# Moving DVE and GpSimd work around a stage boundary, and re-pacing the last stage of a two-layer graph kernel

## The chip, the core and the metric

The kernel runs on one core of a Trainium2 chip. The core has a matrix engine (TensorE, PE in the profile; its weight loads are a row of their own, PEld), three elementwise engines (VectorE = DVE, ScalarE = ACT, GpSimd = POOL) and SyncE (SP), which only issues DMAs. Each engine takes its instructions strictly in order, and an instruction that waits holds up everything behind it on its engine. The metric is the device time of one execution in microseconds (us); lower is better. All arithmetic is float32.

## The reference

Sixteen graphs (B = 16) of 1024 nodes with 256 channels go through two layers, each followed by a residual and a layernorm. Cut to what matters here:

```python
# layer 0
Wg  = adj * similarity(mean over channels)          # 1024 x 1024 per graph
q   = relu((x^T @ Wg) * para)^T ; k, v = split(x @ kv_w)
x1  = layernorm(x + softmax(q k^T * scale) v)       # 4 heads of 64
# layer 1
A   = adj + I
deg = A.sum(0) + A.sum(1) - diag(A) ; dinv = rsqrt(deg)
A_hat = A * dinv[:, None] * dinv[None, :]
agg = A_hat @ x1                                     # the same A_hat for all graphs
h   = relu(batchnorm(agg @ W1.T + b1))               # statistics over all 16*1024 rows
o   = batchnorm(h @ W2.T + b2)
out = layernorm(x1 + o)
```

The two batchnorms cut the kernel into stages: nothing behind one of them can start before the last graph is in front of it.

## The kernel before, in words

A general path stands behind a range check of the softmax denominators and does not run here; the profile is that of `fast_path`. Its stages:

1. **Attention** (to 1692 us). 512 units (graph b, head pair, query half qh, key block m), two units to a "burst", 16 bursts to a graph (u = 0 to 15 in the code). A unit's `scores` are PE matmuls (L926) into a PSUM tile `ps`, ACT's exponential (L931) makes `p` from it, `outputs` are PE matmuls (L947) with `p`, and DVE sums the eight `p` of a group into `acc` (L955 for the first pair, L957 after that). `p` has four buffers, so the exponential of unit i waits for PE and DVE to be done with the `p` of unit i-4. After the eighth unit of a group ACT copies one half of the result (L964) and DVE adds the other half from PSUM (L965, `oT`). A head pair's results are then normalised and added to x (`residual`: DVE L998, PE L1004, DVE L1008, POOL L1013).
2. **The last graph** has no next graph to prepare. Its bursts carry the preparation of A_hat instead, in the table `last`, keyed by u: the adjacency is transposed into eight tiles `ahT` (u = 0 to 7), the degrees and dinv are made (u = 9; dinv goes to DRAM and comes back as a row copied to all partitions, `dinv_row`, L1102 and L1104 on SP), the identity is added on POOL (u = 12, L1109), and `scale_adjacency(m)` multiplies a tile by its column and row of dinv on DVE (L1112). Tiles 0 and 1 are scaled at u = 14, tile 2 inside the last `outputs`, tiles 3 to 7 behind it.
3. **The first aggregate** (`aggregate_first`, L1139, 1695 to 1732 us): for m = 0 to 7, four matmuls into four PSUM banks, of which the two of c = 0 are the banks that the last attention group's `po` had: their first writes wait for L964 and L965. A float32 matmul shows as two instructions. Woven in are `adjacency_sums` (DVE, L693 to L696, four sums per block for the seven-product scheme that the other fifteen graphs use), the last denominators (L977) and the last residuals.
4. **Aggregates and first linear layer** (to 2290 us): seven-product matrix multiplication, paced by PE. Its operands are the sums `aT`, `x1S` (POOL `left_sums`, L686 to L689, one set for each graph) and `wS` (the same helper on W1, once).
5. **Second linear layer** (L1541, to 2515 us): 16 graphs in two halves c of 128 channels. DVE (L1569) or, for the very last half, ACT (L1564) adds the bias b2 and moves the result from PSUM to `o2T`; DVE takes batchnorm statistics from `o2T` (L1573). After the last graph `coefficients2(c)` aggregates them (L1305), DVE and POOL make scale and shift (L1306 to L1310, with POOL's power at L589).
6. **The end** (2515 to 2611 us), a loop over graphs in which `residual2(b)` is PE transposes and additions (L1614, L1629, L1646) with DVE additions and statistics (L1634, L1636, L1652), then the layernorm's ten small instructions (`coefficients`: seven on the engine given, three on POOL); `scale_shift(b)` applies the second batchnorm in place on ACT (L1605); `finish(b)` applies the layernorm on ACT and DVE (L1686, L1680) and stores (L1695 on SP; the last graph in two halves, L1692 on SP and L1693 on ACT's queue). Half of each graph's sum stays in PSUM in one of three `held` buffers until ACT has read it in `finish`. In iteration b come `residual2(b)`, `scale_shift(b + 2)`, `finish(b - 1)`.

PE, ACT and DVE execute in the order in which the code is written. POOL and SP do not: there the tile framework's planner simulates the program and puts each instruction where it finds it ready, program order deciding only between those ready together. In the trace the identity additions, written at u = 12, run on POOL from 1624 us on, between residuals written before and after them.

Of the kernel before, what the change touches and what calls it, by code (L numbers as in the profile page):

```python
# [18 lines left out]
P = 128  # L19
# [496 lines left out]
def fast_path(  # L516
# [43 lines left out]
    def tile_s(name):  # L560
        return psum["s"].tile([P, N], F32, tag="s", name=name)
# [165 lines left out]
    with (  # L727
# [430 lines left out]
        with tc.manual_schedule(engines={mybir.EngineType.PE, mybir.EngineType.Activation, mybir.EngineType.DVE}):  # L1158
# [35 lines left out]
            for u, todo in (  # L1194
                (1, (load_weights,)), (6, (load_x1l, 0)), (9, (degrees,)),
                (10, (transpose_weights, 0)), (11, (transpose_weights, 1)),
                (12, (add_identity,)), (14, (scale_adjacency, 0)),
                (14, (scale_adjacency, 1)),
            ):
                last.setdefault(u, []).append((todo[0], todo[1:]))  # L1200
            for i in range(4):
# [91 lines left out]

    w1T, w2T = wl["w1T"], wl["w2T"]

    def batchnorm(stats, gamma, beta, k, name, eng=nc.gpsimd):


        mv = const.tile([P, k, 2], F32, name=f"{name}_mv")
        sg = const.tile([P, k], F32, name=f"{name}_sg")  # L1300
        sh = const.tile([P, k], F32, name=f"{name}_sh")

        def coefficients(j):
            g, s = sg[:, j : j + 1], sh[:, j : j + 1]
            nc.vector.bn_aggr(mv[:, j, :], stats[:, j].rearrange("p a s -> p (a s)"))  # L1305
            eng.tensor_scalar(g, mv[:, j, 1:2], EPS, None, ALU.add)  # L1306
            rsqrt(g, g, 0.0)
            eng.tensor_tensor(g, g, gamma[:, j : j + 1], ALU.mult)
            eng.tensor_tensor(s, mv[:, j, 0:1], g, ALU.mult)
            eng.tensor_tensor(s, beta[:, j : j + 1], s, ALU.subtract)  # L1310

        return coefficients, sg, sh
# [8 lines left out]
    with (  # L1321
# [9 lines left out]
        def temps(k):  # L1331
# [4 lines left out]

        wS = strt.tile([P, 4, C], F32, name="wS")
        F0, F1 = slice(0, C), slice(C, FH)
        left_sums(
            nc.gpsimd, [wS[:, i, :] for i in range(4)],  # L1340
            w1T[:, 0, F0], w1T[:, 1, F0], w1T[:, 0, F1], w1T[:, 1, F1],
        )

        x1S = {}

# [95 lines left out]
                steps.pop(0)()  # L1441

        x1_sums(1)
        lin = linear1(0)
        for b in range(1, B):
            if 1 < b < B - 1:
# [64 lines left out]
    with tc.tile_pool(name="hl", bufs=2) as hl, tc.tile_pool(name="o2p", bufs=1) as o2p:  # L1511
# [7 lines left out]
            xf[b] = pool.tile([P, NCH, C], F32, tag=tag, name=f"xf_{b}")  # L1519
            nc.sync.dma_start(xf[b], x1_d[b])  # L1520

        coefficients2, sg2, sh2 = batchnorm(bn2_st, cols["g2"], cols["be2"], CC, "bn2", nc.vector)
        hs_of = {0: h0}

        def load_h(b):
# [5 lines left out]
        for b in range(B):  # L1531
            if b + 2 < B:
                load_h(b + 2)
            if b + 1 < B:
                for k in range(HC):
                    scale_shift1(hs_of[b + 1][k], k)
            h = hs_of.pop(b)
            pss = [tile_s(f"po2_{b}_{c}") for c in range(CC)]

            def mm(c, k, hs):  # L1540
                nc.tensor.matmul(  # L1541
                    pss[c][:, hs], w2T[:, k, c * P : (c + 1) * P], h[k][:, hs],
                    start=(k == 0), stop=(k == HC - 1),
                )

            if b == 0:

                for ks in (range(HC // 2), range(HC // 2, HC)):
                    for c in range(CC):
                        for k in ks:  # L1550
                            for hs in (H0, H1):
                                mm(c, k, hs)
            for c in range(CC):
                ps = pss[c]
                last = b == B - 1 and c == CC - 1
                if b:
                    for k, hs in (
                        [(k, hs) for hs in (H0, H1) for k in range(HC)] if last
                        else [(k, hs) for k in range(HC) for hs in (H0, H1)]
                    ):  # L1560
                        mm(c, k, hs)
                if last:
                    for hs in (H0, H1):
                        nc.scalar.activation(  # L1564
                            o2T[b][:, c, hs], ps[:, hs], AF.Identity,
                            bias=cols["b2"][:, c : c + 1],
                        )
                else:
                    nc.vector.tensor_scalar(  # L1569
                        o2T[b][:, c, :], ps, cols["b2"][:, c : c + 1], None, ALU.add  # L1570
                    )
                for half, hs in enumerate((H0, H1)):
                    nc.vector.bn_stats(bn2_st[:, c, 2 * b + half, :], o2T[b][:, c, hs])  # L1573
                if b == B - 1:
                    coefficients2(c)
            if b >= B - 3:
                load_x1(b - (B - 3), xp, "x")
# [7 lines left out]
        with (  # L1585
# [34 lines left out]
            def residual2(b):  # L1620
                xt = xf[b]
                last = b == B - 1
                st = small.tile([P, NCH, 6], F32, tag="ln_st", name=f"st_l1_{b}")
                for pair in range(2):
                    pt = ps_sum.tile([P, HALF], F32, tag="sum", name=f"pf_{b}_{pair}")
                    for j in range(2):
                        n = 2 * pair + j
                        for c in range(CC):
                            nc.tensor.transpose(  # L1629
                                pt[:, j * C + c * P : j * C + (c + 1) * P],  # L1630
                                o2T[b][:, c, n * P : (n + 1) * P], ident,
                            )
                    xs = xt[:, 2 * pair : 2 * pair + 2, :].rearrange("p n c -> p (n c)")
                    nc.vector.tensor_add(xs, pt, xs)  # L1634
                    for n in (2 * pair, 2 * pair + 1):
                        nc.vector.bn_stats(st[:, n, :], xt[:, n, :])  # L1636
                if last:
                    first = coefficients(b, st, M0, nc.vector)
                for pair in range(2, 4):
                    if b:  # L1640
                        add_x1(b, pair)
                    pt = held[b][:, (pair - 2) * HALF : (pair - 1) * HALF]
                    for j in range(2):
                        n = 2 * pair + j
                        for c in range(CC):
                            nc.tensor.matmul(  # L1646
                                pt[:, j * C + c * P : j * C + (c + 1) * P],
                                o2T[b][:, c, n * P : (n + 1) * P], ident,
                                start=False, stop=True, skip_group_check=True,
                            )  # L1650
                for n in range(4, NCH):
                    nc.vector.bn_stats(st[:, n, :], held[b][:, (n - 4) * C : (n - 3) * C])  # L1652
                if last:
                    return first, coefficients(b, st, M1, nc.vector)
                return (coefficients(b, st, slice(0, NCH), nc.gpsimd),) * 2

            def coefficients(b, st, ns, pool):

# [15 lines left out]
            def finish(b, *coeffs):  # L1674
                xt, hx = xf.pop(b), held.pop(b)
                y = o2T[b].rearrange("p c n -> p (c n)").rearrange("p (n c) -> p n c", c=C)
                last = b == B - 1
                for n in (0, 1, 2, 3, 7) if last else (0, 1):
                    rstd, nmr = coeffs[n // 4]
                    nc.vector.tensor_scalar(  # L1680
                        y[:, n, :], hx[:, (n - 4) * C : (n - 3) * C] if n >= 4 else xt[:, n, :],
                        rstd[:, n : n + 1], nmr[:, n : n + 1], ALU.mult, ALU.add,
                    )
                for n in (4, 5, 6) if last else (4, 5, 6, 7, 2, 3):
                    rstd, nmr = coeffs[n // 4]
                    nc.scalar.activation(  # L1686
                        y[:, n, :], hx[:, (n - 4) * C : (n - 3) * C] if n >= 4 else xt[:, n, :],
                        AF.Identity, bias=nmr[:, n : n + 1], scale=rstd[:, n : n + 1],
                    )
                dst = out[b].rearrange("(n p) c -> p n c", p=P)  # L1690
                if last:
                    nc.sync.dma_start(dst[:, M0, :], y[:, M0, :])  # L1692
                    nc.scalar.dma_start(dst[:, M1, :], y[:, M1, :])  # L1693
                else:
                    nc.sync.dma_start(dst, y)  # L1695
                if b in (4, 6):
                    load_x1_pair(b + 6)
                elif b + 7 < B and not 3 <= b < 7:
                    load_x1(b + 7, xp, "x")
# [6 lines left out]
            coeffs = {}  # L1706
            for b in range(B):
                coeffs[b] = residual2(b)
                if b + 2 < B:
                    scale_shift(b + 2)  # L1710
                if b:
                    finish(b - 1, *coeffs.pop(b - 1))
            finish(B - 1, *coeffs.pop(B - 1))
# [43 lines left out]
```

## Time and profile before

| | us |
|---|---|
| median of 3 runs | 2611.93 (2611.75 to 2612.31) |
| profiled execution | 2612.64 |
| its span, first to last instruction | 2610.6 |
| PE busy in the span | 2561.6 (98%) |
| DVE / ACT / POOL busy | 1518.4 / 1201.1 / 356.6 |
| stage borders | attention to 1692, first aggregate to 1732, aggregates and linear 1 to 2290, linear 2 to 2515, end to 2611 |

How to read it. The granted PE clock is 0.996 over the span and falls visibly in two places: 1701 to 1708 us, and behind the last matmul. In the stretch 1692 to 1732 PE is busy for 36.6 of 40.0 us at a mean clock of 0.91; in the end, 73.9 of 96.0 us. Everywhere else in the kernel PE has hardly a gap, so an edit on another engine can only matter where PE waits for that engine, or where PE has no work left.

### The profile page before, as it was taken

How to read it: one execution, taken by the hardware profiler on the slowest of the kernel's cores; microseconds unless marked ns; L12 is line 12 of the kernel's file. 1: busy time of each engine (PE TensorE's matmuls, PEld its weight loads, DVE VectorE, ACT ScalarE, POOL GpSimd, SP SyncE). 2: the span in 40 equal slices, each digit the busy share in tenths (PEclk: the TensorE clock that was granted, in tenths of full speed). 3: DMA queues.
4: the chain of work that ended last, by engine and by line, in shares of the span. 5: the costliest groups of instructions: out<-in, count | busy, mean ns of one | idle time of the engine just before them, and what ended most of it. 6: DMA issues, size and time to landing. Idle time of an engine off the chain costs nothing.

```text
span 2610.6 us, 32351 instructions
## 1 busy us (share of the span) xinstructions
PE 2561.6 (98%) x13158; PEld 1127.4 (43%) x13158; DVE 1518.4 (58%) x1966; ACT 1201.1 (46%) x1478; POOL 356.6 (14%) x427
## 2 busy tenths in 40 slices
PE   9999999999999999999999999999999999999997
PEld 5443443444434434444344344344444444444455
DVE  5375665655756656557566566665655656443368
ACT  6365564664655646646556464611101111143358
POOL 0010110101101101011011010332211222000026
PEclk9999999999999999999999999999999999999999
DMA  4001101011011010110110101022212222254449
GB/s 145 1 10 41 33 10 41 18 26 33 10 41 34 9 41 19 24 33 10 41 34 9 41 19 32 12 79 97 97 65 97 81 97 85 102 200 161 160 165 337
DMA packets 134574, 168.97 MB, mean 65 GB/s; under 512 B 86800, under 2 KB 120080, under 8 KB 124048
## 3 DMA queue, kind: packets, MB, share of 16 engines
q1 hardware_dynamic: 129056, 115.95, 14.3%
q0 software_dynamic: 4832, 50.34, 4.6%
q8 instruction: 105, 1.72, 0.3%
q10 hardware_dynamic: 528, 0.52, 0.1%
q14 instruction: 53, 0.43, 0.1%
HBM read 99.36 MB, written 67.44 MB: 64 GB/s over the span
## 4 chain that ended last, share of the span: by engine, by line
PE 86%; DVE 9%; ACT 3%; issue 1%; DMA 0%; POOL 0%; DVEq 0%; POOLq 0%; ACTq 0%
PE ps L926 16%; PE po L947 16%; PE pg L829 16%; PE po L1541 8%; PE pv L879 5%; PE b_agg L1371 4%; PE c_agg L1371 4%; PE pk L866 3%; PE a_agg L1371 2%; PE b_h L1403 2%; PE c_h L1403 2%; PE pxT L790 1%; PE den L977 1%; PE a_h L1403 1%; PE pagg L1139 1%; PE pg L851 1%
## 5 line engine op out<-in xcount | busy, mean ns | idle before, releaser
L931 ACT ACTIVATE p<-ps 128x1024 f32<-128x1024 f32 x512 | 496.8, 1024 | 183.9 <-PE ps L926 152.6
L957 DVE TENSOR_TENSOR acc<-acc,p 128x1024 f32<-128x1024 f32 x384 | 487.4, 1269 | 122.4 <-ACT p L931 94.1
L926 PE MATMUL ps<-qT,kT 64*64 64x512 f32 x4096 | 490.8, 592 | 0.7 <-DVE qT L838 0.3
L947 PE MATMUL po<-p,v 64*64 64x512 f32 x4096 | 487.9, 589 | 0.0
L829 PE MATMUL pg<-wg,x 128*128 128x512 f32 x960 | 420.9, 594 | 0.0
L1013 POOL TENSOR_TENSOR x<-x,o 128x512 f32<-128x512 f32 x64 | 122.2, 1910 | 1164.7 <-DVE o L1008 1164.7
L947 PEld LDWEIGHTS po<-p,v 64*64 64x64 f32 x4096 | 160.0, 133 | 280.2 <-issue 271.3
L829 PEld LDWEIGHTS pg<-wg,x 128*128 128x128 f32 x960 | 178.9, 190 | 221.5 <-issue 208.5
L926 PEld LDWEIGHTS ps<-qT,kT 64*64 64x64 f32 x4096 | 152.0, 133 | 281.5 <-issue 250.4
L1541 PE MATMUL po<-hl,w12T 128*128 128x512 f32 x512 | 220.0, 592 | 0.8 <-ACT hw L1493 0.8
L838 DVE SCALAR_TENSOR_TENSOR qT<-pg,para_s 128x1024 f32<-128x1024 f32 (+1 forms) x34 | 39.2, 1161 | 236.2 <-PE pg L829 234.9
L819 DVE SCALAR_TENSOR_TENSOR wg<-wg,adj_s 128x1024 f32<-128x1024 f32 x128 | 162.1, 1278 | 21.7 <-ACT wg L815 21.7
L810 ACT ACTIVATE wg<-crow,ccol 128x1024 f32<-128x1024 f32 x128 | 147.1, 1150 | 7.9 <-DMA crow<-c 7.9
L1541 PEld LDWEIGHTS po<-hl,w12T 128*128 128x128 f32 x512 | 97.2, 190 | 123.6 <-issue 120.1
L815 ACT ACTIVATE wg<-wg 128x1024 f32<-128x1024 f32 x128 | 136.3, 1065 | 1.7
L1478 ACT ACTIVATE hl<-hl,bn_sh,bn_sg 128x1024 f32<-128x1024 f32 x64 | 74.1, 1230 | 133.0 <-DMA hl<-h 131.7
L879 PE MATMUL pv<-kvw_s,xT 128*128 128x256 f32 x512 | 126.8, 390 | 6.7 <-ACT kT L870 6.7
L965 DVE TENSOR_TENSOR oT<-po,oT 128x512 f32<-128x512 f32 x64 | 44.2, 691 | 145.8 <-ACT oT L964 145.8
L866 PE MATMUL pk<-xT,kvw_s 128*128 128x512 f32 x256 | 121.9, 598 | 3.3 <-ACT v L884 3.3
L1569 DVE TENSOR_SCALAR o<-po,col_b 128x1024 f32<-128x1024 f32 x31 | 39.8, 1284 | 133.3 <-PE po L1541 133.3
L624 ACT ACTIVATE x<-x,nm_l,rs_l 128x256 f32<-128x256 f32 x128 | 64.8, 588 | 108.0 <-POOL nm_l L620 108.0
L841 ACT ACTIVATE qT<-qT 128x1024 f32<-128x1024 f32 (+1 forms) x34 | 34.2, 1008 | 174.5 <-DVE qT L838 174.5
(179 smaller groups left out, 2750.8 us busy)
## 6 DMA issues: line engine op xcount, KB each, us to landing
h<-hw POOLq DMA_DIRECT2D x16, 2048.0 KB, 6.9
hl<-h SPq DMA_DIRECT2D x15, 2048.0 KB
x<-x POOLq DMA_DIRECT2D x16, 1024.0 KB, 4.2
x1l<-x SPq DMA_DIRECT2D x16, 1024.0 KB
xf<-x SPq DMA_DIRECT2D x16, 1024.0 KB
x<-in_x_dram SPq DMA_DIRECT2D x15, 1024.0 KB
out_dram<-o SPq DMA_DIRECT2D x15, 1024.0 KB
crow<-c SPq DMA_DIRECT2D x15, 512.0 KB
```

What stands on the lines that cost most here:

```text
L810: nc.scalar.activation(w, s["crow"], AF.Abs, bias=s["ccol"][:, n : n + 1])
L815: nc.scalar.activation(w, w, AF.Tanh, scale=0.5)
L819: nc.vector.scalar_tensor_tensor(w, w, 1.0, adj_s[:, n, :], op0=ALU.subtract, op1=ALU.mult)
L829: nc.tensor.matmul(s["pg"][:, hs], xt[:, n, c * P : (c + 1) * P], s["wg", n][:, hs], start=(n == 0), stop=(n == NCH - 1),)
L866: nc.tensor.matmul(ps, kvw_s[:, c, kc * P : (kc + 1) * P], s["xT"][:, c, hs], start=(c == 0), stop=(c == CC - 1),)
L879: nc.tensor.matmul(pt[:, j * C : (j + 1) * C], s["xT"][:, c, n * P : (n + 1) * P], kvw_s[:, c, C : 2 * C], start=(c == 0), stop=(c == CC - 1),
L926: nc.tensor.matmul(ps[kh * D : (kh + 1) * D, hd * HALF : (hd + 1) * HALF], kT[r, pr, ks], qT[r, pr, qh * HALF : (qh + 1) * HALF], start=Tr ...
L931: nc.scalar.activation(p, ps, AF.Exp)
L947: nc.tensor.matmul(g["po"][kh][hd * D : (hd + 1) * D, :], s["v"][r, m, h * D : (h + 1) * D], p[r, hd * HALF : (hd + 1) * HALF], start=(m = ...
L957: nc.vector.tensor_add(g["acc"], g["acc"], p)
L1371: nc.tensor.matmul(ps, left, right, start=(start and i == 0), stop=(i == NCH // 2 - 1), skip_group_check=True,)
L1541: nc.tensor.matmul(pss[c][:, hs], w2T[:, k, c * P : (c + 1) * P], h[k][:, hs], start=(k == 0), stop=(k == HC - 1),)
```

## The change

Five edits, with no change of what is computed:

- `scale_adjacency(0)` and `(1)` move from burst u = 14 to u = 12 on DVE.
- The four `left_sums` that make `wS` on POOL are written after `x1_sums(1)`, not before it.
- The second batchnorm's statistics read the matmul's result in PSUM, without b2; `batchnorm` adds b2 to the mean with one more small instruction per half. The very last half of channels gets a PSUM tile of its own for each half of its nodes, so that its two halves are separate.
- In the end, `scale_shift` runs three graphs ahead and not two, and the layernorm coefficients of graph 0 are made on DVE and not on POOL.
- The last graph's eighth block is applied by ACT and not by DVE; the stores of graphs 12 to 14 are issued as two halves, blocks 4 to 7 first.

```diff
-                (12, (add_identity,)), (14, (scale_adjacency, 0)),
-                (14, (scale_adjacency, 1)),
+                (12, (add_identity,)), (12, (scale_adjacency, 0)), (12, (scale_adjacency, 1)),
...
-    def batchnorm(stats, gamma, beta, k, name, eng=nc.gpsimd):
+    def batchnorm(stats, gamma, beta, k, name, eng=nc.gpsimd, bias=None):
...
             rsqrt(g, g, 0.0)
+            if bias is not None:
+                eng.tensor_tensor(
+                    mv[:, j, 0:1], mv[:, j, 0:1], bias[:, j : j + 1], ALU.add
+                )
             eng.tensor_tensor(g, g, gamma[:, j : j + 1], ALU.mult)
...
-        left_sums(
-            nc.gpsimd, [wS[:, i, :] for i in range(4)],
-            w1T[:, 0, F0], w1T[:, 1, F0], w1T[:, 0, F1], w1T[:, 1, F1],
-        )
...
         x1_sums(1)
+        left_sums(
+            nc.gpsimd, [wS[:, i, :] for i in range(4)],
+            w1T[:, 0, F0], w1T[:, 1, F0], w1T[:, 0, F1], w1T[:, 1, F1],
+        )
         lin = linear1(0)
...
-            pss = [tile_s(f"po2_{b}_{c}") for c in range(CC)]
+            pss = [tile_s(f"po2_{b}_{c}") for c in range(CC if b < B - 1 else CC - 1)]
+            last_ps = [tile_o(f"po2_last_{half}") for half in range(2 if b == B - 1 else 0)]
+
+            def half_ps(c, hs):
+                if last_ps and c == CC - 1:
+                    return last_ps[0 if hs == H0 else 1]
+                return pss[c][:, hs]
...
                         nc.scalar.activation(
-                            o2T[b][:, c, hs], ps[:, hs], AF.Identity,
+                            o2T[b][:, c, hs], half_ps(c, hs), AF.Identity,
...
-                    nc.vector.bn_stats(bn2_st[:, c, 2 * b + half, :], o2T[b][:, c, hs])
+                    nc.vector.bn_stats(bn2_st[:, c, 2 * b + half, :], half_ps(c, hs))
...
-                return (coefficients(b, st, slice(0, NCH), nc.gpsimd),) * 2
+                pool = nc.gpsimd if b else nc.vector
+                return (coefficients(b, st, slice(0, NCH), pool),) * 2
...
-                for n in (0, 1, 2, 3, 7) if last else (0, 1):
+                for n in (0, 1, 2, 3) if last else (0, 1):
...
-                for n in (4, 5, 6) if last else (4, 5, 6, 7, 2, 3):
+                for n in (4, 5, 6, 7) if last else (4, 5, 6, 7, 2, 3):
...
+                elif b >= B - 4:
+                    nc.sync.dma_start(dst[:, M1, :], y[:, M1, :])
+                    nc.sync.dma_start(dst[:, M0, :], y[:, M0, :])
                 else:
                     nc.sync.dma_start(dst, y)
...
                 coeffs[b] = residual2(b)
-                if b + 2 < B:
-                    scale_shift(b + 2)
+                if b == 0:
+                    scale_shift(2)
+                if b + 3 < B:
+                    scale_shift(b + 3)
```

More of the change, by code (lines that the diff above doesn't have):

```diff
@@ L1520, in load_x1 @@
             nc.sync.dma_start(xf[b], x1_d[b])
-        coefficients2, sg2, sh2 = batchnorm(bn2_st, cols["g2"], cols["be2"], CC, "bn2", nc.vector)
+        coefficients2, sg2, sh2 = batchnorm(
+            bn2_st, cols["g2"], cols["be2"], CC, "bn2", nc.vector, cols["b2"]
+        )
         hs_of = {0: h0}
@@ L1537, in fast_path @@
             h = hs_of.pop(b)
-            pss = [tile_s(f"po2_{b}_{c}") for c in range(CC)]
+            pss = [tile_s(f"po2_{b}_{c}") for c in range(CC if b < B - 1 else CC - 1)]
[4 more added lines that the diff above has]
+                return pss[c][:, hs]
             def mm(c, k, hs):
                 nc.tensor.matmul(
-                    pss[c][:, hs], w2T[:, k, c * P : (c + 1) * P], h[k][:, hs],
+                    half_ps(c, hs), w2T[:, k, c * P : (c + 1) * P], h[k][:, hs],
                     start=(k == 0), stop=(k == HC - 1),
@@ L1553, in fast_path @@
             for c in range(CC):
-                ps = pss[c]
                 last = b == B - 1 and c == CC - 1
@@ L1569, in fast_path @@
                     nc.vector.tensor_scalar(
-                        o2T[b][:, c, :], ps, cols["b2"][:, c : c + 1], None, ALU.add
+                        o2T[b][:, c, :], pss[c], cols["b2"][:, c : c + 1], None, ALU.add
                     )
                 for half, hs in enumerate((H0, H1)):
-                    nc.vector.bn_stats(bn2_st[:, c, 2 * b + half, :], o2T[b][:, c, hs])
+                    nc.vector.bn_stats(bn2_st[:, c, 2 * b + half, :], half_ps(c, hs))
                 if b == B - 1:
@@ L1677, in finish @@
                 last = b == B - 1
-                for n in (0, 1, 2, 3, 7) if last else (0, 1):
+                for n in (0, 1, 2, 3) if last else (0, 1):
                     rstd, nmr = coeffs[n // 4]
                     nc.vector.tensor_scalar(
-                        y[:, n, :], hx[:, (n - 4) * C : (n - 3) * C] if n >= 4 else xt[:, n, :],
-                        rstd[:, n : n + 1], nmr[:, n : n + 1], ALU.mult, ALU.add,
+                        y[:, n, :], xt[:, n, :], rstd[:, n : n + 1], nmr[:, n : n + 1],
+                        ALU.mult, ALU.add,
                     )
-                for n in (4, 5, 6) if last else (4, 5, 6, 7, 2, 3):
+                for n in (4, 5, 6, 7) if last else (4, 5, 6, 7, 2, 3):
                     rstd, nmr = coeffs[n // 4]
```

## The prediction

> **What bounds the kernel now.** I read the busy times first, then the clock by stretches, then the waits, the chain and the timelines of the two places that the diff touches.
>
> ```profile
> PE 2561.6 (98%) x13158; PEld 1127.4 (43%) x13158; DVE 1518.4 (58%) x1966; ACT 1201.1 (46%) x1478; POOL 356.6 (14%) x427
> ```
>
> PE is the bound almost everywhere, so I look only for places where it waits or runs slowly. The waits from 1690 to 1735 us name one, and the busy times by stretch (PE, PEld, DVE, ACT, POOL, then PE clock) show what it drags behind it:
>
> ```profile
> PE pagg L1139 <- DVE oT L965: 3.3, 1, 3.3
> ```
> ```profile
> 1701.00:1703.00 2.00, 1.44 (x2) 0.83 (x3) 2.00 (x3) 0.00 (x0) 0.00 (x0) 0.50 0.79 266
> 1705.00:1707.00 2.00, 2.00 (x4) 0.82 (x3) 2.00 (x2) 0.00 (x0) 2.00 (x2) 0.50 0.00 0
> 1707.00:1709.00 2.00, 2.00 (x5) 0.60 (x3) 2.00 (x2) 0.00 (x0) 2.00 (x2) 0.81 0.00 0
> ```
>
> The first aggregate's fourth matmul waits 3.27 us for DVE's `oT`, and PE then runs at half clock until about 1707.5. The chain of waits shows what DVE did meanwhile and what the slow clock cost; POOL's timeline shows its neighbour:
>
> ```profile
> 1693.62 1.27 DVE ahT L1112
> 1694.89 1.15 DVE acc L957
> ...
> 1696.13 3.13 DVE acc L957
> ...
> 1700.83 0.69 DVE oT L965
> ...
> 1701.56 7.63 PE pagg L1139 x10
> ```
> ```profile
> 1696.06 0.74 POOL L686 TENSOR_TENSOR wS<-w12T 128x256 f32<-128x256 f32 x1
> ```
>
> Ten matmul instructions take 7.63 us; the 24 behind them take 10.50, or 0.43 each. At that pace ten are 4.3 us: the slow clock costs 3.3. So the place holds 3.27 + 3.3 = 6.6 us, no more. Of the DVE time in front of `oT`, 2.4 us are the two scalings of u = 14, and 1.9 are one L957 stretched from 1.2 to 3.13 beside the `wS` sums.
>
> The second place is the border before the end and the end itself:
>
> ```profile
> 2514.92 0.70 ACT o L1564
> ...
> 2515.64 1.30 DVE bn_st L1573 x2
> ...
> 2516.96 1.03 DVE bn_mv L1305
> ...
> 2519.42 0.82 ACT o L1605
> ```
> ```profile
> PE held L1614 <- ACT o L1686: 3.1, 8, 0.4
> ...
> DVE st_l L1652 <- PE held L1646: 0.9, 4, 0.2
> ```
>
> Here the chain runs through ACT's bias addition into the statistics. Later it is DVE's (4.73 us per graph in the timeline, from L1634 to L1634) until ACT, at 5.05 us per graph, falls so far back that the `held` buffers come free late.
>
> **Scaling at u = 12.** It issues two DVE instructions (L1112, 2.47 us together) and no DMA, and passes no queue but DVE's. It removes them from before `oT`. But at u = 12 DVE arrives at 1683.60, and their operand `dinv_row` is still on its way (last columns: DMA share, GB/s):
>
> ```profile
> 1684.00:1684.50 0.50, 0.50 (x12) 0.17 (x6) 0.50 (x1) 0.50 (x2) 0.00 (x0) 1.00 1.02 360
> 1684.50:1685.00 0.50, 0.50 (x8) 0.15 (x4) 0.43 (x2) 0.50 (x1) 0.00 (x0) 1.00 0.61 189
> 1685.00:1686.00 1.00, 1.00 (x11) 0.32 (x4) 0.00 (x0) 1.00 (x3) 0.00 (x0) 1.00 0.00 0
> ```
>
> Its last bytes move at about 1684.8. For the load of x1l(1) the last bytes to POOL's start on it were 0.6 us, so I put the row at 1685.3: a new DVE wait of 1.7 us. Queued behind it are L955 of units 24 and 25, the two residual steps, and L957 of units 26 and 27; ACT's exponentials of units 28 to 31 wait for those, for they need the `p` buffers. I walk it. Scalings 1685.3 to 1687.7. L955 ends 1688.9, not 1684.8; the exponential of unit 28 moves from 1687.91 to 1688.95, harmless. L1008 at 1689.1, POOL's L1013 (1.27), L1008 again at 1691.2, then L957 of 26 to 1693.05 and of 27, stretched to 2.1 beside POOL as it is now, to 1695.2 (now 1692.50). So the exponential of unit 30 starts at 1693.1 and of 31 at 1695.3, not at 1691.30 and 1692.59. PE's outputs of 28 and 29 still end at 1693.6; then it waits 0.5 for unit 30 and 1.3 for 31, and attention ends 1.7 us late at 1697.2. Three L957 (3.5) bring DVE to 1698.7 and `oT` to 1699.4. PE reaches its fourth aggregate matmul at 1699.8: no wait there. Result: ten instructions end at 1699.8 + 4.3 = 1704.1 against 1709.19, **5.1 us won**.
>
> [...] The row: a gap of 3.27 us ended with the clock at 0.50 from 1701, some 2.7 us after PE's last work; a 1.95 us gap before 2520.28 left it at 1.00. [...] the 3.3 us might be absent in other executions, and the edit would be worth 3.27 - 1.7 = 1.6; by the row, 5.1. The unprofiled median lies only 0.7 us below the profiled execution, which leaves little room for executions without the drop, so I take the row. [...]
>
> What is late next: DVE has scaling 2, the last L957, five scalings and sixteen sums still to do, 22.5 us from `oT` to L998 now. With `wS` and `x1S(1)` both beside them I expect 24.5, so L998 comes at about 1724, as now, while PE ends the aggregate at 1726.8 and not 1731.87. The statistics behind it then reach POOL at 1731.5 and ACT's `last_apply` (4.04) at 1735.0; the copy p_h behind that on ACT ends at 1739.6, where PE wants it at 1739.5. I charge 0.2 to 0.4. **First place: 4.7 us.**
>
> **wS later.** Four POOL instructions, no DMA. `x1S(1)` is not ready until its load (1704.95); `wS` is ready at 1696. As the planner takes what is ready, I expect the order to stay. It costs or gains: if it stays, nothing; if it moves, the 2 to 3 us of stretching go from scaling 2 to the adjacency sums, where DVE's lead over PE hides them as above. `wS` is first read at 1740.8 (1735.7 then), 15 us after its latest end. Nil; without that cover, each us of DVE is one us at p_h.
>
> **Statistics from PSUM.** Not on the path for 31 of 32 halves: DVE adds 1.3 us to a PSUM tile's life, and PE is 6.87 us in the other tile. For the last half the first 512 nodes are done 1.7 us before PE ends, and the second needs one L1573 (0.65) after 2514.90, not ACT's 0.70 and two L1573 (1.30). L1305 starts at 2515.6, not 2516.96: 1.3 won. The added addition of b2 (0.16) lies in DVE's 0.66 us wait for POOL's power. ACT's three L1605 of c = 0 end at 2518.2 and let the next start there: **1.2 us**. [...]
>
> ```profile
> L1636 DVE BATCH_NORM_STATS2 st_l<-xf 128x6 f32<-128x256 f32 x64 | 24.1, 419 | 1.1
> L1652 DVE BATCH_NORM_STATS2 st_l<-held 128x6 f32<-128x256 f32 x64 | 22.6, 417 | 0.9 <-PE held L1646 0.9
> ```
>
> `held` is PSUM, `xf` SBUF: no difference. [...]
>
> **The longer lead.** Graph 0's coefficients put seven small operations on DVE, 0.99 us for the same seven at 2595.5, and DVE is the bound here: a loss of 1.0. POOL's idle time was not worth anything. In return `finish(0)` can start when two more L1605 are done: 2518.2 + 7.18 + 2.4 = 2527.7, not 2529.14, with one more graph scaled, so ACT's lead grows by 1.4 + 2.4 = 3.8 us. It loses 0.32 per graph; `held` stalls PE at a lag of some 2.1 and DVE at some 3.1, which now comes at graph 11, the last one with a scaling before it. At DVE's pace the loop, 4.1 + 4.1 + 14 x 4.73 + 0.9 from 2520.87, would end at 2596.2; it ended at 2597.83. Of these 1.6 I count 1.4 back. Net with the 1.0: **0.4**.
>
> **Last block and stores.** ACT's last three L1686 start 0.7 us after POOL's coefficients (2600.94), behind DVE's block 7. With four they end at 2602.95, not 2603.12: 0.2 won. The DMA engines are full (331 to 350 GB/s) from 2602 to 2606.8; halves let graph 14's blocks 4 to 7 start 1.1 us earlier, so this queue does not hold the earlier last store. The three additional SP issues cost 0.4 each with SP idle. **0.2.**
>
> **Sum.** 4.7 + 1.2 + 0.4 + 0.2 = 6.5. The profiled execution, span 2610.6 and 2.0 around it, becomes 2612.64 - 6.5 = 2606.1; the median lies 0.71 under it: 2611.93 - 6.5 = **2605.4 us**. About 0.2%, 5.2 us, is what a measurement here can tell from no change.
>
> **Rivals.** (1) *DVE becomes the bound of the first aggregate*: two more us of contention, or of wait for the row, go through p_h or the `p` buffers to PE one to one; and the end wins only the border's 1.2. For it: L998 without slack. Against: PE's last 10 us of aggregate need nothing more of DVE. 2.7 + 0.8 gives 3.5: 2608.4. (2) *Clean*: the row is there at 1684.9 or POOL does not stretch L957, so attention ends on time; 6.6 + 2.6: 2602.7. For it: the gaps of 0.5 and 1.3 are small differences of walked times. (3) *Slower: the row is late.* DVE stands at 1683.60 until it lands. Each us past 1685.3 is a us of PE, and once the wait for unit 31 (1.3 now) reaches 3.3, the clock falls again (3.3). The trace bounds it: at 1692.42 the scaling ran with no wait shown. The worst is 7.1 + 3.3 - 6.5 = 3.9: 2615.8; slower from 3.2 us of lateness (6.5 - 3.2 - 3.3). Against it: the DMA's bytes end by 1685. (4) *No change shows*, if the slow clock is the profiler's: 1.6 + 1.8 = 3.4, as (1).
>
> **How the numbers follow.** Main case 0.54 (2603.4 to 2607.6), clean 0.18, DVE-bound or no clock loss 0.23, late row 0.05. Eight in ten: 2602.3 to 2609.2, leaving out the late row and the outer ends of (1) and (2). Faster by over 0.2% needs 5.2: clean, and nearly nine tenths of the main case, 0.66; slower by over 0.2% only if the late row meets other losses, 0.02; within, 0.32.
>
> **What would show it.** Right: no wait for L965 and clock 1.00 through 1700 to 1710; L1112 with a DMA wait near 1684; two PE gaps under 1.5 us at L947; L1305 starting 0.7 us after the last L1541; no DVE wait for `held`. Wrong: a PE gap over 3 us before 1700, POOL's `wS` elsewhere with DVE slower, or PE waiting for p_h at about 1740.

## The result, and the profile after

The change makes the kernel 0.18% faster: 2607.23 us median (2606.06 to 2607.93, 21 runs) against 2611.66 (2610.35 to 2612.38, 21 runs), ratio 0.9982 with a 95% interval of 0.9976 to 0.9989. That is 4.4 us; the forecast was 6.5 us, 2605.4. The profiled execution has a span of 2605.1 us and took 2607.23.

The page's busy times, and the waits from 1680 to 1735 us of the kernel after (engine, what waited, what released it: total us, times, longest):

```profile
PE 2560.0 (98%) x13158; PEld 1126.9 (43%) x13158; DVE 1515.6 (58%) x1974; ACT 1201.7 (46%) x1479; POOL 355.8 (14%) x420
```
```profile
PE po L947 <- ACT p L931: 1.1, 1, 1.1
DVE ahT L1112 <- DMA dinv_row<-dinv: 1.0, 1, 1.0
```

PE's wait of 3.3 for `oT` is gone. DVE now waits for the row of dinv, and PE has one new gap of 1.1 in front of the last unit. The busy times by stretch show the clock at 1.00 where it stood at 0.50 (same columns as before):

```profile
1701.00:1703.00 2.00, 2.00 (x6) 0.88 (x5) 2.00 (x2) 0.00 (x0) 1.99 (x2) 1.00 0.85 340
1705.00:1707.00 2.00, 2.00 (x11) 0.61 (x11) 2.00 (x3) 0.56 (x1) 0.00 (x0) 1.00 0.77 274
1707.00:1709.00 2.00, 2.00 (x7) 0.80 (x6) 2.00 (x2) 0.03 (x1) 0.27 (x1) 1.00 0.53 221
```

The chain of waits runs as walked in the prediction: the scalings, the residual with its POOL step, two L957 of which the second is long, one exponential, PE's last outputs, and then the aggregate without a break.

```profile
1687.31 1.28 DVE ahT L1112
...
1690.71 1.28 POOL x L1013
...
1693.95 2.12 DVE acc L957
...
1696.15 1.03 ACT p L931
...
1697.23 1.09 PE po L947 x8
1698.32 7.06 PE pagg L1139 x16
```

At the border before the end, the timeline of DVE and ACT (start, duration, instruction; in brackets the idle time before it and what ended it). PE's last L1553, formerly L1541, ends at 2511.40:

```profile
2511.44 0.69 ACT L1575 ACTIVATE o<-po_last,col_b 128x512 f32<-128x512 f32 x1 [2.75 <-PE po_last L1553]
2512.16 0.70 DVE L1584 BATCH_NORM_STATS2 bn_st<-po_last 128x6 f32<-128x512 f32 x1 [2.03 <-ACT o L1575]
2512.90 1.02 DVE L1305 BATCH_NORM_AGGREGATE bn_mv<-bn_st 128x2 f32<-128x192 f32 x1
2515.35 9.44 ACT L1616 ACTIVATE o<-o,bn_sh,bn_sg 128x512 f32<-128x512 f32 x9 [0.68 <-DVE bn_sh L1314]
```

DVE reads PSUM now, as the edit wants, but by the bracket it starts only when ACT is done with the same tile. In the end itself the waits for `held` are shorter:

```profile
PE held L1625 <- ACT o L1698: 1.9, 5, 0.4
DVE st_l L1663 <- PE held L1657: 0.4, 2, 0.2
```

### The profile page after: what moved, and what is told of

Its sections match the earlier page's. It is cut to its first block, busy times and chain, and to the rows that moved or that the text cites. A ratio compares the mean times of both kernels' runs of the same rounds, so it can differ in the third digit from the quotient of the medians.

```text
span 2605.1 us, 32348 instructions
## 1 busy us (share of the span) xinstructions
PE 2560.0 (98%) x13158; PEld 1126.9 (43%) x13158; DVE 1515.6 (58%) x1974; ACT 1201.7 (46%) x1479; POOL 355.8 (14%) x420
## 4 chain that ended last, share of the span: by engine, by line
PE 86%; DVE 9%; ACT 3%; issue 1%; DMA 1%; POOL 0%; DVEq 0%; POOLq 0%; ACTq 0%
PE ps L926 16%; PE pg L829 16%; PE po L947 16%; PE po L1553 8%; PE pv L879 5%; PE b_agg L1371 4%; PE c_agg L1371 4%; PE pk L866 3%; PE a_agg L1371 2%; PE b_h L1403 2%; PE c_h L1403 2%; PE pxT L790 1%; PE a_h L1403 1%; PE den L977 1%; PE pagg L1139 1%; PE pg L851 1%
## 5 line engine op out<-in xcount | busy, mean ns | idle before, releaser
L957 DVE TENSOR_TENSOR acc<-acc,p 128x1024 f32<-128x1024 f32 x384 | 485.7, 1265 | 122.6 <-ACT p L931 94.1
L926 PE MATMUL ps<-qT,kT 64*64 64x512 f32 x4096 | 490.8, 592 | 0.7 <-DVE qT L838 0.3
L926 PEld LDWEIGHTS ps<-qT,kT 64*64 64x64 f32 x4096 | 152.0, 133 | 281.5 <-issue 250.2
L1553 PE MATMUL po<-hl,w12T 128*128 128x512 f32 x496 | 213.1, 592 | 0.8 <-ACT hw L1497 0.8
L1553 PEld LDWEIGHTS po<-hl,w12T 128*128 128x128 f32 x496 | 94.2, 190 | 119.8 <-issue 116.0
L965 DVE TENSOR_TENSOR oT<-po,oT 128x512 f32<-128x512 f32 x64 | 44.3, 692 | 145.8 <-ACT oT L964 145.8
```

The lines of the kernel that those rows point to most:

```text
L926: nc.tensor.matmul(ps[kh * D : (kh + 1) * D, hd * HALF : (hd + 1) * HALF], kT[r, pr, ks], qT[r, pr, qh * HALF : (qh + 1) * HALF], start=Tr ...
L957: nc.vector.tensor_add(g["acc"], g["acc"], p)
L1553: nc.tensor.matmul(half_ps(c, hs), w2T[:, k, c * P : (c + 1) * P], h[k][:, hs], start=(k == 0), stop=(k == HC - 1),)
```

## The experiments

Each gain below is the difference of the medians from the runs of the kernel before that stood beside it. Each ratio's 95% interval reaches about 1.8 to 2.2 us to either side, so differences between two experiments of less than 1 us are read together with their profiles, not alone.

### The kernel before again, twice

Nothing is edited; both runs are of the same code, the second for one more profile.

> The kernel before, unchanged: a second profile of it, and its times against itself. Theory A (the drop of the granted clock to 0.50 from 1701 belongs to the 3.3 us wait for L965): the second profile shows the wait of about 3.3 for L965 and then some 6 us of clock 0.50 again, ten L1139 in about 7.6 us, and the first aggregate ends about 35 us after unit 31's last L947, as in the first. Theory B (whether a gap of that length drops the clock depends on where it falls): the same wait, but clock 1.00 after it, and ten L1139 in about 4.3 us. Start of the first graph's attention: the two profiles so far differ by 1.46 us already there in identical code; if that is chance, this profile falls anywhere between. Time: 1.000 of before within 0.0008.

> The kernel before, unchanged, for one more profile of the stretch at 1700. So far the clock stood at 0.50 for 6.7, 3.4 and 3.4 us with the same wait of 3.3. Theory B (a fixed stretch with free edges): again 3.4 or 6.7, and nothing between, the ten L1139 in 6.0 to 6.3 or in 7.6. Theory A (the first profile is typical): 6.7.

Measured: 2611.43 us, ratio 0.9999 (0.9991 to 1.0007), and 2612.60 us in the single run for the third profile. The wait for L965 is the same in every profile of this code; what follows it is not. PE's timeline of the first profile, of the second, and of the third (the ten instructions behind the wait):

```profile
1701.56 7.63 PE L1139 MATMUL pagg<-ahT,x1l 128*128 128x512 f32 x10 [3.27 <-DVE oT L965]
```
```profile
1703.07 6.26 PE L1139 MATMUL pagg<-ahT,x1l 128*128 128x512 f32 x10 [3.26 <-DVE oT L965]
```
```profile
1702.95 6.25 PE L1139 MATMUL pagg<-ahT,x1l 128*128 128x512 f32 x10 [3.27 <-DVE oT L965]
```

At full clock ten are 4.3, so the slow ten lost 3.3 us in the execution that the prediction had, and 1.9 in the two others. (About 0.2 of each is the restart and not the clock: behind a shorter wait and at clock 1.00, ten take 4.56, see "Half of the scalings".) The busy times of the second profile show where it was slow (the PE clock is the third column from the end):

```profile
1700.90:1704.20 3.30, 1.13 (x3) 0.65 (x4) 3.30 (x4) 0.00 (x0) 0.44 (x1) 0.99 0.48 139
1704.20:1707.50 3.30, 3.30 (x5) 1.24 (x5) 3.30 (x4) 0.00 (x0) 1.17 (x1) 0.50 0.44 184
```

PE had been back at work for 1.1 us when the clock fell. With stretches of 0.5 us, and each edge placed inside its stretch by the mean clock there, the slow time is 3.41 us in both repeats, and 6.83, twice that, in the first profile. Neither theory of the first expectation had this; it is Theory B of the second.

The profiles also begin differently: the first scores matmul (L926) of the first graph starts at 70.67 in the first profile, and at 72.19 and 72.05 in the two others. The first eight L802, in the first and in the second profile, show where this arises:

```profile
8.30 3.60 PE L802 MATMUL crow<-xT,ncmat 128*128 128x512 f32 x8
```
```profile
8.50 4.92 PE L802 MATMUL crow<-xT,ncmat 128*128 128x512 f32 x8
```

In the first profile all of them start 0.43 us apart, the pace of L1139 at full clock. In the second the first four start 0.86, 0.85 and 0.85 us apart, the pace of L1139 in the slow stretch at 1701, and from 11.54 on they come at 0.43 too. The clock column reads 1.00 there only because the trace's record of the granted clock begins later, with a change to 1.00 at 7.94 us in the first profile and at 11.16 and 10.86 in the two others; what lies before the first record counts as 1.00. So PE starts at half clock by the pace in the second profile, and in the first it starts slow too (the first twelve L790, up to 7.6 us, have a median of 418 ns, the later ones 273), for a time that differs from one execution to the next. In all thirteen profiles kept here this first change lies between 7.94 and 11.16 us, and the first L926 between 70.6 and 72.2, and a later change goes with later scores, by about half of the difference.

### The scalings alone

```diff
-                (12, (add_identity,)), (14, (scale_adjacency, 0)),
-                (14, (scale_adjacency, 1)),
+                (12, (add_identity,)), (12, (scale_adjacency, 0)), (12, (scale_adjacency, 1)),
```

> Before, with the two scalings moved from u = 14 to u = 12 and nothing else. Theory A (trace sum): 3.3 of wait and 3.3 of slow clock go, 1.1 of gap at L947 and 0.2 come: 4.7 to 5.2 us faster in the median, 2606.9. Theory B (the slow clock is there in only part of the executions): 1.6 to 3.5 us faster, 2608.2 to 2610.0. Theory C (what is won at the boundary is given back at p_h or later): under 1.5 us.

Measured: 2608.53 us against 2611.64, ratio 0.9988 (0.9982 to 0.9995): 3.1 us, as Theory B has it. From the first graph's first L926 to the first `a_agg` matmul of the aggregates takes 1656.7 us here and 1656.6 with the whole change; the kernel before takes 1661.9 in the first profile and 1660.5 in each of the two others. So the profiles say 5.2 by the first and 3.8 by the others. That the two new figures agree also says that the weight sums, which this experiment leaves in their old place, are worth nothing. Whether Theory B's reason also holds, executions without any slow clock, is taken up below.

### Half of the scalings

```diff
-                (12, (add_identity,)), (14, (scale_adjacency, 0)),
+                (12, (add_identity,)), (12, (scale_adjacency, 0)),
```

> Before, with only the first of the two scalings moved to u = 12: PE's wait for L965 shrinks from 3.27 by what one scaling takes, to 1.9 to 2.3. Theory A (my step: the drop follows 2.7 us after PE's last work): a gap of two us has no drop, ten L1139 take 4.3 to 4.4; the kernel is 1.2 + 1.7 to 3.3 faster than before, 2607.2 to 2608.8. Theory B [...]: some executions still drop; the profile may show the clock at 0.50 for 3.4 us and ten L1139 in about 6, and the gain is 1.2 to 2.9.

Measured: 2608.79 us against 2612.06, ratio 0.9989 (0.9981 to 0.9997): 3.3 us, the same as with both. The expected wait of 1.9 to 2.3 was wrong. It is 1.0:

```profile
1699.85 4.56 PE L1139 MATMUL pagg<-ahT,x1l 128*128 128x512 f32 x10 [1.02 <-DVE oT L965]
```

The three L957 ahead of `oT` take 4.27 here and 6.10 before: one instruction moved took 1.27 from the path, and with another timing beside POOL the sums were also 1.8 shorter, of which the wait for the row took some back. The clock stays at 1.00. Since neither theory's gap occurred, this run doesn't tell them apart; the stretch from the first L926 to `a_agg`, 1656.7 us as with both scalings moved, shows that after one there was nothing more to win from the second.

### The end alone

The scalings and the weight sums stay as before; the rest of the change is in.

> Before, with the statistics from PSUM, the longer lead with graph 0's coefficients on DVE, four of the last block on ACT and the stores in halves; the scalings and the weight sums stay where they were. Theory A (profiles of before and after from PE's last L1541 to the end of the span: 95.7 and 93.7): 2.0 us faster, 2609.7. Theory C (the first place was worth all of the 4.4 us, the end nothing): within 0.5 of before. Either way the border should show DVE's L1584 of H1 waiting for ACT's L1575 of H1 as in the profile after, with L1305 starting 1.4 to 1.5 after PE's last matmul (2.06 before), not 0.7.

Measured: 2609.56 us against 2611.64, ratio 0.9994 (0.9985 to 1.0002): 2.1 us by the medians, 1.6 by the ratio, with an interval that just includes none. So the times lean to Theory A but don't exclude Theory C. The profiles speak for A: from PE's last matmul to the end of the span takes 93.7 us, against 95.2 to 95.7 in the three of the kernel before. Its profile has the unmoved scalings too, with a clock loss of 1.7 (the ten L1139 take 6.04), so four profiles with this wait now read 3.3, 1.9, 1.9 and 1.7. The border is as expected: its L1305 starts 1.49 after PE's last matmul, behind ACT's addition.

### The lead, and graph 0's coefficients

```diff
-                pool = nc.gpsimd if b else nc.vector
-                return (coefficients(b, st, slice(0, NCH), pool),) * 2
+                return (coefficients(b, st, slice(0, NCH), nc.gpsimd),) * 2
```

> The change, with graph 0's coefficients back on POOL. Theory A (DVE is the bound of the end and these seven operations, 1.0 us, are on its path): 0.8 to 1.0 us faster than the change, 2606.3. Theory B (finish of graph 0 then starts 1.2 us later on ACT and ACT's lead is what decides): ACT's lead shrinks by 1.2, DVE's wait for held grows from 0.4 to up to 1.6, and the time is the same within 0.3 or worse by 0.2.

The second experiment has this edit and the old lead:

```diff
-                if b == 0:
-                    scale_shift(2)
-                if b + 3 < B:
-                    scale_shift(b + 3)
+                if b + 2 < B:
+                    scale_shift(b + 2)
```

> The change, with two graphs scaled ahead as before and graph 0's coefficients on POOL: the whole step of the longer lead undone. Theory A (my sum: 1.4 won back and 1.0 lost): 0.4 us slower than the change, 2607.6, with DVE waiting about 0.9 in all for held. Theory B (profiles: DVE's wait for held fell by only 0.5 for the 1.0 spent): 0.3 to 0.5 us faster than the change. Theory C (the end's gain of 2 us is all from the lead): 1.2 us slower.

Measured: 2606.37 and 2606.74 us against 2611.65 (ratios 0.9981, 0.9973 to 0.9989 for both): 0.9 and 0.5 faster than the change by the medians. That is Theory A for the first and Theory B for the second. From PE's last L1553 to the end of DVE's last statistics takes 82.7 us with the change and 82.3 in both experiments. With the coefficients on POOL DVE's wait for `held` is back at 0.9, and still the end is no later:

```profile
PE held L1625 <- ACT o L1697: 2.7, 7, 0.4
DVE st_l L1663 <- PE held L1657: 0.9, 4, 0.2
```

So the seven operations on DVE cost more than the waits that they shorten; the lead as a whole is a small loss. Its size, 0.3 to 0.5, is at the limit of what the runs resolve, and so is what scaling three graphs ahead wins by itself (0.4 by the medians, nothing by the profiles).

### Whole stores

```diff
-                elif b >= B - 4:
-                    nc.sync.dma_start(dst[:, M1, :], y[:, M1, :])
-                    nc.sync.dma_start(dst[:, M0, :], y[:, M0, :])
```

> The change, with the last graphs' stores in one piece again (the last graph's own two stores are as they were). Theory A (the DMA engines are full until about 2602, and halves let the stores of graphs 12 to 14 begin 1.1 earlier): 0.4 to 0.8 us slower than the change. Theory B (the transfers are hidden behind the last block's computation, and the last store alone sets the end): within 0.2 of the change.

Measured: 2608.47 us against 2611.65, ratio 0.9987 (0.9981 to 0.9994): 1.2 us slower than the change, more than either theory had. The last store's issue on ACT is at the same time in both (2599.09 here, 2599.19 with the change), but the span ends at 2606.4, not 2605.1. The busy times by stretch of the change first, then with whole stores (last two columns: DMA share, GB/s):

```profile
2595.00:2598.00 3.00, 0.00 (x0) 0.00 (x0) 2.10 (x7) 1.21 (x3) 1.72 (x3) 0.50 0.89 287
2602.00:2604.00 2.00, 0.00 (x0) 0.00 (x0) 0.00 (x0) 0.00 (x0) 0.00 (x0) 0.50 0.04 15
```
```profile
2595.00:2598.00 3.00, 0.00 (x0) 0.00 (x0) 2.00 (x7) 1.21 (x3) 1.71 (x3) 0.50 0.48 158
2602.00:2604.00 2.00, 0.00 (x0) 0.00 (x0) 0.00 (x0) 0.00 (x0) 0.00 (x0) 0.50 0.50 166
```

With whole stores the DMA engines are half idle from 2595 to 2598, where graph 14's one store waits for its last block, and then full at 343 GB/s until past 2602. Halves move about 1.3 us of transfer into the idle time.

### Two versions beyond the change

The second scaling is put behind `oT`, where only tile 1 of the aggregate waits for it. In the last `outputs`:

```diff
+                scale_adjacency(1)
                 scale_adjacency(2)
...
-                (12, (add_identity,)), (12, (scale_adjacency, 0)), (12, (scale_adjacency, 1)),
+                (12, (add_identity,)), (12, (scale_adjacency, 0)),
```

> The change, with only the first scaling at u = 12 and the second one put right behind oT (L965) of the last unit pair, ahead of the third scaling. Theory A (the two gaps of PE at L947, of 0 to 1.1 us, come from DVE being held up 1.0 for the row and 2.5 for the scalings): the gap of 1.1 shrinks to under 0.3 and the kernel is 0.8 to 1.1 us faster than the change, 2606.2 to 2606.5. Theory D (the aggregate's fifth matmul pair then waits for the second scaling, or DVE gets to L998 1.2 later): the gain is lost again, within 0.3 of the change; then PE shows a wait for L1112 at about 1700 or for p_h at about 1740.

Measured: 2606.53 us against 2611.64, ratio 0.998 (0.9972 to 0.9987). The gap of 1.1 is gone, and a smaller one is new:

```profile
1700.74 3.67 PE L1140 MATMUL pagg<-ahT,x1l 128*128 128x512 f32 x8 [0.60 <-DVE ahT L1113]
```

From the first L926 to `a_agg` it is 1656.3 us, 0.3 less than with the change: Theory A for the gap, Theory D for about half of its worth, since the two scalings behind `oT` take 3.50 us, beside POOL's `wS`.

On top of this, DVE's last statistics go ahead of ACT's bias additions (the two blocks of code change places for the last block):

```diff
+                for half, hs in enumerate((H0, H1)):
+                    nc.vector.bn_stats(bn2_st[:, c, 2 * b + half, :], half_ps(c, hs))
                 if last:
                     for hs in (H0, H1):
                         nc.scalar.activation(
...
-                for half, hs in enumerate((H0, H1)):
-                    nc.vector.bn_stats(bn2_st[:, c, 2 * b + half, :], half_ps(c, hs))
```

> The kernel with the split scalings (e4_scaling_split), and in the last block DVE's two statistics are put ahead of ACT's two additions of the bias; both read the same PSUM tiles. Theory A (one of two readers of a PSUM tile is held back until the other is done, in the order of the program): DVE's last statistics start 0.05 after PE's last matmul, the aggregation 0.75, not 1.45; ACT's last addition now starts 0.7 later and its three scalings of c = 0 behind it end at about 3.9 after PE's last matmul, so ACT starts c = 1 no earlier than before: 0 to 0.2 faster than e4. Theory B (ACT isn't held back by DVE): ACT's c = 1 starts at 3.2 to 3.3 after PE's last matmul, not 3.95, and the kernel is 0.6 to 0.7 us faster than e4, 2605.9.

Measured: 2606.08 us against 2611.65, ratio 0.9978 (0.997 to 0.9986). The waits turn round with the order of the code:

```profile
2509.88 0.70 DVE L1579 BATCH_NORM_STATS2 bn_st<-po_last 128x6 f32<-128x512 f32 x1 [1.31 <-PE po_last L1554]
2510.61 0.69 ACT L1582 ACTIVATE o<-po_last,col_b 128x512 f32<-128x512 f32 x1 [1.33 <-DVE bn_st L1579]
2510.61 1.02 DVE L1306 BATCH_NORM_AGGREGATE bn_mv<-bn_st 128x2 f32<-128x192 f32 x1
2511.20 11.97 ACT L1617 ACTIVATE o<-o,bn_sh,bn_sg 128x512 f32<-128x512 f32 x12
```

Now L1306 starts 0.75 after PE's end at 2509.86, but ACT has no gap left between c = 0 and c = 1, so its own three scalings set the start of c = 1: Theory A. The median moved 0.45, more than its 0 to 0.2; from PE's last matmul to the end of the span it is 93.6 us, with the split scalings alone 93.8.

The last version adds graph 0's coefficients on POOL to this.

> The change, with the second scaling behind L965, DVE's last statistics ahead of ACT's additions of the bias, and graph 0's coefficients on POOL. If the three gains add (0.7, 0.45 and 0.86 against the change): 2605.2. If they share a cause (ACT's lead at graph 0 is cut twice by 1.2 of POOL): 2605.6 to 2606.1.

Measured: 2606.51 us against 2612.06, ratio 0.998 (0.9972 to 0.9987). Against its own runs of the kernel before that is 5.55 us, the same as without the coefficients (5.57). Set on the earlier runs (2611.65) it is 2606.1, the upper end of what was expected for gains that share a cause. They don't add: from PE's last matmul to the end it is 93.6 us in both. No version here is faster than statistics first with the split scalings.

## Why the prediction was right, and where it was wrong

The measured 2607.23 lies in the eight-in-ten range of 2602.3 to 2609.2. The gain of 0.18% does not reach the 0.2% that the prediction gave a chance of 0.66; it gave 0.32 to what came.

**Scaling at u = 12: the mechanism held, the term for the clock was mis-sized.** The row of dinv was expected at 1685.3 and the attention 1.7 late. Set to the same start (the profile after begins 1.45 later), the scaling starts at 1684.7 and the attention ends 1.4 late. In place of two gaps of 0.5 and 1.3 PE has one of 1.1, with the clock at 1.00 behind it. There is no wait for L965, and p_h cost PE nothing. By the very profile that the sum was made on, the place gave 5.3, not 4.7. But the sum took "the slow clock costs 3.3" for a property of the kernel. It was 1.7 to 1.9 in the three other profiles, so the place held 5.1 us to win, not 6.6, and the forecast becomes 3.2 on the forecast's own losses, or 3.6 to 3.9 by the profiles. The scalings alone measured 3.1. If half of the slow time in which PE was busy is taken off, all four profiles with the wait give 1658.8 us from the first L926 to `a_agg`, against 1656.6 with the change: by this estimate the edit is worth 2.1 us in an execution without a slow stretch, 3.6 to 3.9 with one, and 5.3 with two.

The prediction also gave the worth without any slow clock, 1.6, and put it aside for the 5.1 of its one profile; the measured 3.1 lies between. With the same wait of 3.25 to 3.27 the slow time was 3.41 us in three profiles and 6.83 in one, so its length in a single execution is a draw, and the prediction's profile was one draw. The mean clock of whole executions suggests that it was a rare one: over 131 executions of the kernel before it reads 0.996, as in the first profile, in 4, 0.997, as in those with 3.41 us of slow clock, in 83, and 0.998 in 44. Whether these 44 had no drop at all is not shown, since the slow time behind PE's last work varies too (9.6 to 12.5 us in the profiles). With this wait the clock fell in every one of the four profiles. In the second profile the 3.41 us ahead of the drop hold 1.1 us of PE work.

**The argument that chose the row was unsound.** The prediction said that the median, 0.71 under the profiled execution, "leaves little room for executions without the drop". Two deviations had cancelled: that execution lost 1.5 us more to the clock, and it began its attention 1.5 us earlier than both repeats. Both go with the times at which its clock changed. It went to full clock at 7.94 us, early, and fell 1693.01 us later (the same distance in all four profiles), at 1700.95, when PE still had 0.6 us to wait; it stayed at 0.50 for 6.83. In the repeats both changes lie about 3 us later (11.16 and 1704.17 in the second profile): the start is slow for longer, and PE is already back at work when the clock falls, for 3.41. But one does not always bring the other: the end-alone profile has an early start (8.10), a drop 0.4 us before PE resumes, and only 3.41 us of slow clock. What decides between 3.41 and 6.83 these runs do not show. Rival 4, "no change shows, if the slow clock is the profiler's", had the wrong reason, but with 3.4 for the whole change it came nearer to the measured 4.4 than the 6.5 of the main case.

**wS later: nothing, as forecast, and for its reason: the order stayed.** POOL runs the four sums from 1699.62 to 1704.66, still ahead of `x1S(1)` at 1708.73.

**Statistics from PSUM: 0.6, not 1.2** (read off the profiles; no run has this edit alone). The step that failed is "the second needs one L1573 (0.65) after 2514.90". It took two readers of one PSUM tile to run side by side. In this program the second is held until the first is done (L1584 begins at 2512.16, L1575 ends at 2512.13), so L1305 came 1.5 after PE's end and not 0.7. ACT starts c = 1 3.95 after PE's end instead of 4.52. The change of order shows that c = 0 on ACT would have been next in the way. That the PSUM source itself costs DVE nothing (417 ns in the forecast's group on `held`, 419 in that on `xf`) is right: L1584 on PSUM has a median of 685 ns, the old L1573 on SBUF 686.

**The longer lead: -0.3 to -0.5, not +0.4.** The 1.0 for the seven operations came as costed (2521.02 to 2522.04). The step that failed is "of these 1.6 I count 1.4 back". The `held` waits that the lead was to remove fell from 0.9 to 0.4 for DVE; the stretch from ACT's c = 1 to DVE's last statistics rose from 78.4 to 78.7 us.

**Last block and stores: 1.3 to 1.7, not 0.2.** ACT's four L1698 behind the coefficients give the forecast 0.2 (from DVE's last statistics to ACT's store 5.31 before, 5.11 after). From that store's issue to the end of the span it was 7.4 before and is 5.9 now, 1.5 less; over all profiles it is 7.0 to 7.4 with whole stores and 5.9 to 6.1 with halves. The run with whole stores puts 1.2 on the halves by the medians, 1.4 by its profile. The prediction named the 1.1 us of earlier start and that the DMA engines are full to the end, and then booked neither: the last transfer here, behind a full queue, gained what had left the queue before it.

That the end came out near its forecast was luck: its errors cancelled almost wholly (0.6 - 0.3 + 1.7 = 2.0 by the profile, forecast 1.8, measured alone 2.1). The clock was the error that didn't cancel. The parts measured alone sum to 5.2, 0.8 more than the change itself. That lies inside the intervals, and these runs don't settle whether the parts share something.

## What to carry to other kernels

A slow-clock stretch in one profile is one draw (6.83 us here, against 3.41 in three others): profile the unchanged kernel two or three times, and line the profiles up at a common matmul, before you price it. At the end of a kernel, look at the DMA share by stretch ahead of the last store: idle share there, followed by a full queue, is time that smaller stores can win (1.2 us of about 1.3 here). An engine freed from waiting for data still waits for other readers where the program orders them (DVE's last statistics began 0.76 us after PE's end here, when ACT was done with the tile); look who else reads the tile.

## What the runs showed of the hardware that was not expected

- With PE waiting 3.25 to 3.27 us in the same place, the granted clock stood at 0.50 for 3.41, 3.41, 3.41 and 6.83 us (the first of the end-alone profile, then the two repeats, then the first profile), beginning between 0.6 us before and 1.1 us after PE resumed. Of the first 3.41 us of slow clock PE was busy for 82% in the first profile and for 89% in the end-alone profile, where full clock then came. At the start of the kernel full clock came 2.9 us after PE's first work in the first profile (5.00 to 7.94) and 6.3 us after it in the second (4.87 to 11.16). What decides the length is not shown.
- The times between changes of the clock fit whole multiples of one length. Half of the first profile's slow stretch of 6.827 us goes 496 times into the 1693.01 us ahead of it, 261 times into the 890.88 behind it, and 757 times into the 2583.89 of full clock in the kernel after, to within 0.13 us each.
- Identical code reaches the first graph's scores at 70.6 to 72.2 us, a spread of 1.6 us where the times of the kernel before spread over 2.2 in one set of 51 executions. The pace of the first L802 (0.85 to 0.86 us apart among the first four of the second profile, 0.43 from 11.54 us on) shows that PE starts at half clock; the profile's clock column does not.
- Beside POOL's weight sums DVE's two-input instructions took longer: in the version with the split scalings, the two L1113 behind `oT` take 3.50 us from 1698.76, with `wS` on POOL from 1697.81 to 1702.85, while the one at 1685.50 takes 1.28.
